# A decoder layer on one core: the weighting products as a stream of their own, a later read of x, an earlier mask load, and a changed account in the planner

## The chip, the core and the metric

The kernel runs on one core of one Trainium2 chip. The core has TensorE (matrix products, written into PSUM), VectorE, ScalarE and GpSimd (elementwise work and reductions), SyncE, which here only issues DMAs, and 16 DMA engines. The metric is the device time in microseconds, from one launch to its end. In the profile's rows PE is TensorE's products, PEld its weight loads, DVE is VectorE, ACT is ScalarE, POOL is GpSimd and SP is SyncE; a q behind a name (SPq) is that engine's sequencer.

## What is computed

A pre-norm decoder layer in float32 over x of shape (4, 1024, 256), with three residual parts. Cut to what matters:

```python
def attn(x):                     # 16 heads of 16, causal
    Q = (x @ Wq.T + bq).reshape(b, s, H, hd)
    K = (x @ Wk.T + bk).reshape(b, s, H, hd)
    V = (x @ Wv.T + bv).reshape(b, s, H, hd)
    Qt = einsum('bqhf,hfg->bqhg', Q, W_cross)
    K_mixed = einsum('hfg,bkhg->bkhf', M, K)     # M: shift_weights on diagonals
    scores = gt * (Qt . K) + (1 - gt) * (Q . K_mixed)
    attn = softmax(where(causal, scores * hd ** -0.5, -inf))
    return (attn @ V) @ Wo.T + bo

x = x + attn(layernorm(x))
x = x + cross_attention(layernorm(x), ctx, mask)   # 77 context rows, mask (4, 1024, 77)
x = x + w_down(silu(w_gate(n)) * w_up(n))          # n = layernorm(x), hidden 768, integer weights
```

## The kernel before

**Chunks.** The work goes in eight chunks, four batches b of two halves n, each of 512 rows (CH). Causality makes the second half of a batch cost twice the keys: n = 0 has 4 key blocks of 128, n = 1 has 8. Heads are taken in four groups of four (NG).

**Parts of a chunk.** `project` (L769) normalises the chunk's rows, transposes them and makes q, k and v. The rows of q and k are split into a rounded part and a remainder (hi, lo) and laid out by DMAs between parts of SBUF (`spread`, L713; eight DMAs at L727 for each half of q or of k, 128 KB each). `maxima` (L825) makes all scores once to find the row maxima: products at L853 and, on the diagonal, L861, reduced on VectorE at L866; `shift` (L732) turns the maxima. `attend` (L890) makes the scores again transposed, two pieces for each key block (L936, L942, diagonal L949), takes the exponential on ScalarE into an `es` buffer (L955), and weighs the values with it (L979, the inner function `weigh`). After the last key block of a group the sums are copied out (`normalise`, L659), transposed back and divided (`quotients`, L998; products at L668); after the last group the output projection follows (`out_proj`, L687; VectorE adds it to x at L711). `cross_attention` (L1043) and `ffn` (L1178) follow for the chunk; the FFN's products are at L1220 and L1254, and GpSimd makes the remainder of the hidden rows at L1231, into an `es` buffer too.

**Order of the weighing before.** `weigh` lags the scores by one key block, inside the attention stream: two score pieces, then the weighing of the block before them, and so on; quotients and output projection stand in the same stream, so that the scores of the next chunk come after the output projection of this one. x is read again (L906) for the residual sum when the chunk's attention begins; GpSimd adds the output bias to it (L909).

**Buffers.** PSUM has three `pair` buffers (scores, projections, FFN) and two `single` ones (sums). SBUF has six `es` buffers, two for each key block of a group, three `x` buffers, each held from the read of x to the end of the chunk's FFN, two `mk` buffers (masks) and the small ones.

**The order.** The prologue, up to L358, is in program order on every engine: weights come in on SP's and ScalarE's queues (L211 to L224), x01 (the second chunk's rows) last. Then a planner written into the kernel, `weave` (L458), orders TensorE's work while the program is built. Each part is a `Stream` of pieces; a piece states its TensorE time, the engines that it uses afterwards, the buffers that it takes and frees, a condition and an earliest time. `weave` always picks the piece that can start first in its account; streams that come first in the list win ties within 0.01 us, and a per-chunk list, LATES, shifts a stream's bids. A change of the array's shape (`mode`: rows of 64, columns of 32, whole) is charged 0.11 us. Once the maxima of the second group have begun ("begun"), only TensorE's order is written by the planner; before that VectorE's is too. The other engines' orders, SP's DMA issues among them, are the scheduler's own: it takes instructions in an order of its choice, ahead of their place in the program where nothing that they depend on holds them.

**Masks.** The mask of a batch is loaded by `load_mask` (L1013): the first in `late_weights` (L526, call at L532), the next ones in the cross attention. `load_cross` (L1017) reduces it (L1038) and scales it (L1040).

Of the kernel before, what the change touches and what calls it, by code (L numbers as in the profile page):

```python
# [8 lines left out]
F32 = mybir.dt.float32  # L9
# [3 lines left out]
U8 = mybir.dt.uint8  # L13
AF = mybir.ActivationFunctionType
ALU = mybir.AluOpType
# [4 lines left out]
P = 128  # L20
# [7 lines left out]
def tile_decoder_layer(  # L28
# [163 lines left out]


# [30 lines left out]
    x01 = x_rows(0, 1)  # L224

# [205 lines left out]
    tensor = {"end": 0.0, "mode": None}  # L431
# [26 lines left out]
    def weave(*streams, until=None):  # L458
        while True:
            live = [s for s in streams if s.next is not None]  # L460
            if not live or until in flags:
                return
            can = []
            for s in live:
                p = s.next
                if p["cond"] is not None and not p["cond"]():
                    continue
                t = max(
                    tensor["end"], p["at"], *(slots[k].when(c) for k, c in p["take"].items()), 0.0
                )  # L470
                if p["pe"] and p["mode"] != tensor["mode"]:
                    t += SWITCH
                if p["use"] and p["take"]:

                    eng, us = p["use"][0]
                    t = max(t, busy[eng].start(t + p["pe"], us) - p["pe"] - 1.0)
                if t < 1.0e8:
                    can.append((t + (s.lates[s.chunk] if s.lates else 0.0), t, s))
            assert can, [s.next for s in live]
            soon = min(c[0] for c in can) + WAIT  # L480
            _, t, s = next(c for c in can if c[0] <= soon)
            p = s.next
            s.got = {k: [slots[k].take() for _ in range(c)] for k, c in p["take"].items()}
            s.end = t + p["pe"]
            if p["pe"]:
                tensor.update(end=s.end, mode=p["mode"])
            for token in p["free"]:
                give(token, s.end)
            s.done = s.end
            for eng, us in p["use"]:  # L490
                s.done = busy[eng].run(s.done + LATE, us)
            s.next = next(s.pieces, None)
# [33 lines left out]
    def late_weights(st):  # L526
# [5 lines left out]
        load_mask(0)  # L532
# [236 lines left out]
    def project(st, b, n):  # L769
# [4 lines left out]
        else:  # L774
# [6 lines left out]
            normal_rows(xn, *row_scales(xn))  # L781
            yield piece(
# [6 lines left out]
        for c in range(NC):  # L789
# [8 lines left out]
            if c == 0:  # L798
                for i in range(QT):
                    if i % 2 == 0:  # L800
                        yield piece(
                            2.0, use=[("ACT", 1.8)] if i else [],
                            **({} if i else {"pair": 1, "v": 1}),
                        )
                        if i == 0:
                            t_pair, t_v = st.got["pair"], st.got["v"][0]
                            vs = qk.tile(
                                [P, QT, H * V1 + W - V1], F32, tag="v", name="vs", bufs=NQ
                            )
                            nc.gpsimd.memset(vs, 1.0)  # L810
                            t = pair().rearrange("p a (i d) -> p (a i) d", d=D)
# [77 lines left out]

    def attend(st, b, n):  # L890


        nat = t_nat = None
        nk = (n + 1) * QT
        lag = []
        tails = []
        for g in range(NG):
            c = g // 2
            if g % 2 == 0:
                yield piece(0.0, cond=lambda: (b, n, c) in shifts and (b, n) in vT and "selections" in flags)  # L900
                ms, at, t_ms = shifts.pop((b, n, c))
                if g == 0:
                    yield piece(0.0, x=1, use=[("DMA", 4.0)])
                    xt = xpool.tile([P, QT, D], F32, tag="x", name="x", bufs=3)
                    xs[b, n] = xt, st.got["x"][0]
                    nc.sync.dma_start(  # L906
                        xt, x[b, n * CH : (n + 1) * CH, :].rearrange("(t p) d -> p t d", p=P)
                    )
                    nc.gpsimd.tensor_tensor(  # L909
                        xt, xt, bo_b.unsqueeze(1).to_broadcast([P, QT, D]), ALU.add  # L910
                    )
# [4 lines left out]
            acc = []  # L916
            for kb in range(nk):
                kc, ki = divmod(kb, QT)
                k = kT[b, kc, c][0]
                vs, t_v, v_at = vT[b, kc]  # L920
# [4 lines left out]
                for p in range(2):  # L925
                    yield piece(
                        0.04 + w * 8.2e-4 + (0.11 if diag else 0.0), mode="rows", pair=1, es=1,
                        at=at,
                        use=[("ACT", 0.1 + w * 1.85e-3)],
# [29 lines left out]
                    ready = max(st.done + LATE, v_at)  # L959
                if g == 2 and n == NQ - 1 and kb == 0:  # L960
                    flags.add(("half", b))


                if g == NG - 1 and n == NQ - 1 and ki == QT - 1:
                    toks = toks + [t_v]

                def weigh(g=g, kb=kb, ki=ki, lo=lo, w=w, both=both, vs=vs, acc=acc, toks=toks,
                          ready=ready):
                    last = kb == nk - 1
                    yield piece(  # L970
                        0.03 + w * 1.77e-3, at=ready, free=toks, mode="cols",
                        use=[("ACT", 0.6)] if last else [],
                        **({"single": 1} if kb == 0 else {}), **({"f2": 1} if last else {}),
                    )
                    if kb == 0:
                        acc += [single(), st.got["single"][0]]
                    for jj in range(4):
                        h = 4 * g + jj
                        nc.tensor.matmul(  # L979
                            acc[0][W * jj : W * (jj + 1), lo:],  # L980
                            vs[:, ki, V1 * h : V1 * h + W], both[jj // 2][:, jj % 2, lo:],
                            start=(kb == 0), stop=last,
                        )
                    if last:
                        give(acc[1], st.done)
                        tails.append((normalise(acc[0]), st.got["f2"], st.done + LATE, g))

                lag.append(weigh)
                if len(lag) > 1:
                    yield from lag.pop(0)()  # L990
                if tails and kb == 1:
                    nat, t_nat = yield from quotients(st, tails.pop(), nat, t_nat)
        yield from lag.pop()()
        nat, t_nat = yield from quotients(st, tails.pop(), nat, t_nat)
# [16 lines left out]
    masks, mks = {}, {}  # L1011

    def load_mask(b):  # L1013
        mks[b] = xpool.tile([P, NT, S2], U8, tag="mk", name="mk", bufs=2)
        nc.sync.dma_start(mks[b], mask[b].rearrange("(t p) s -> p t s", p=P))
# [254 lines left out]
    def every(part, lates, chunks=range(NQ)):  # L1270
# [11 lines left out]
        [-0.05, 0.00, 0.00, 0.00, -0.09, 0.00, -0.11, 0.02],  # L1282
        [0.00, 0.00, -0.09, 0.00, 0.00, 0.00, 0.00, -0.48],
        [0.00, 0.00, 0.00, 0.00, 0.00, 0.00, 0.00, 0.00],
        [-3.63, 0.00, 0.00, 0.00],
        [0.74, 0.00, 0.00, 0.15],
        [0.00, -0.15, -0.34, 0.00, 0.00, 0.41, 0.00, 0.00],
    )
    streams = [
        every(maxima, LATES[0]), every(cross_attention, LATES[1]), every(attend, LATES[2]),  # L1290
        *(every(project, LATES[3 + n], [n]) for n in range(NQ)),
        Stream(late_weights), *(Stream(lambda st, m=m: load_ffn(st, m)) for m in range(3)),
        every(ffn, LATES[5]),
# [64 lines left out]
```

## Time and profile before

| what | us |
|---|---|
| median of 3 runs | 1239.33 (1238.6 to 1239.84) |
| profiled execution | 1236.36 |
| its span, first to last instruction | 1234.6 |
| TensorE busy | 1108.7 |
| VectorE busy | 729.8 |
| ScalarE busy | 561.2 |
| GpSimd busy | 130.5 |
| mean granted TensorE clock | 0.956 of full speed |
| 16 DMA engines, share of the span, SP's queue | 38.7% |

The costliest groups of instructions; the columns are line, engine, operation, output and inputs, shape, count, then busy time, mean ns of one, idle time of the engine just before them and what ended most of it:

```profile
L866 DVE TENSOR_REDUCE mt<-pair 128x2 f32<-128x1024 f32 (+3 forms) x384 | 352.6, 953 | 96.0 <-PE pair L861 60.8
L955 ACT ACTIVATE es<-pair 128x1024 f32<-128x1024 f32 (+3 forms) x384 | 300.2, 811 | 227.8 <-PE pair L949 158.1
L853 PE MATMUL pair<-k,q 64*128 64x512 f32 (+3 forms) x768 | 163.8, 432 | 39.9 <-DVE mt L866 15.1
L936 PE MATMUL pair<-q,k 64*128 64x512 f32 (+3 forms) x768 | 163.7, 423 | 18.5 <-DVE mt L866 9.7
L979 PE MATMUL single<-es,vs 128*32 128x512 f32 (+3 forms) x1536 | 163.3, 498 | 0.0
```

A busy time of TensorE is modelled at its end and is no proof of full speed; idle time of an engine that is not the bound costs nothing. The profile's slices and stretches give the granted clock beside the busy time, so that slow stretches can be told from empty ones.

### The profile page before, as it was taken

The numbers are of one execution on the slowest core, as the hardware profiler recorded it, in microseconds if no ns is written. First come the engines' busy times: TensorE is split into PE (matmuls) and PEld (weight loads), VectorE is DVE, ScalarE is ACT, GpSimd is POOL, SyncE is SP. The second block draws the span as 40 slices with busy tenths as digits, with TensorE's granted clock in tenths as the row PEclk, the third lists the DMA queues.
The fourth block names the chain that finished last, engine by engine and source line by source line (L and its number), as shares of the span: only waits on it lengthen the run. The fifth ranks groups of instructions, "written<-read, shape, count | busy, mean of one in ns | idle before, by whom it ended". The sixth has DMA issues, their size and how long they took to land. (4 is left out here: it accounts for less than half of the span.)

```text
span 1234.6 us, 22019 instructions
## 1 busy us (share of the span) xinstructions
PE 1108.7 (90%) x9059; PEld 683.7 (55%) x9059; DVE 729.8 (59%) x1247; ACT 561.2 (45%) x801; POOL 130.5 (11%) x138
## 2 busy tenths in 40 slices
PE   6489999999789999999899899899999899897975
PEld 4355545556556457557656456556656555456664
DVE  4577686254677867245777863652667746516443
ACT  3035455644343564653343555355344364572421
POOL 3230000001200003001200000201110000002112
PEclk9689999999999999999899899899899999998987
DMA  6973425457242014566533016363823314005000
GB/s 119 162 140 79 66 43 70 69 86 99 39 72 35 6 43 71 88 86 98 71 56 52 6 26 103 56 92 57 104 37 53 48 38 49 18 1 67 19 35 19
DMA packets 65437, 76.44 MB, mean 62 GB/s; under 512 B 22450, under 2 KB 39398, under 8 KB 65331
## 3 DMA queue, kind: packets, MB, share of 16 engines
q1 hardware_dynamic: 64227, 74.62, 38.7%
q8 instruction: 73, 1.20, 0.5%
q10 hardware_dynamic: 1104, 0.35, 0.1%
q14 instruction: 33, 0.27, 0.1%
HBM read 15.28 MB, written 9.33 MB: 20 GB/s over the span
## 5 line engine op out<-in xcount | busy, mean ns | idle before, releaser
L866 DVE TENSOR_REDUCE mt<-pair 128x2 f32<-128x1024 f32 (+3 forms) x384 | 352.6, 953 | 96.0 <-PE pair L861 60.8
L955 ACT ACTIVATE es<-pair 128x1024 f32<-128x1024 f32 (+3 forms) x384 | 300.2, 811 | 227.8 <-PE pair L949 158.1
L853 PE MATMUL pair<-k,q 64*128 64x512 f32 (+3 forms) x768 | 163.8, 432 | 39.9 <-DVE mt L866 15.1
L936 PE MATMUL pair<-q,k 64*128 64x512 f32 (+3 forms) x768 | 163.7, 423 | 18.5 <-DVE mt L866 9.7
L979 PE MATMUL single<-es,vs 128*32 128x512 f32 (+3 forms) x1536 | 163.3, 498 | 0.0
L853 PEld LDWEIGHTS pair<-k,q 64*128 64x128 f32 x768 | 76.8, 192 | 122.8 <-DVE mt L866 44.5
L942 PE MATMUL pair<-ms,sel 64*128 64x512 f32 (+3 forms) x768 | 135.8, 350 | 0.0
L936 PEld LDWEIGHTS pair<-q,k 64*128 64x128 f32 x768 | 73.5, 188 | 106.8 <-issue 38.4
L1231 POOL TENSOR_TENSOR hT<-h,hT 128x512 fp32r<-128x512 f32 x48 | 61.3, 1277 | 336.3 <-ACT hT L1230 310.4
L1153 ACT ACTIVATE es<-pair 77x1024 f32<-77x1024 f32 x64 | 63.1, 1018 | 35.6 <-PE pair L1151 35.1
L942 PEld LDWEIGHTS pair<-ms,sel 64*128 64x128 f32 x768 | 74.6, 191 | 2.8
L1254 PE MATMUL pair<-wdT,hT 128*128 128x256 f32 x384 | 61.9, 311 | 14.8 <-POOL hT L1231 4.1
L861 PE MATMUL pair<-cm_qk,id 64*128 64x64 bf16 (+1 forms) x1024 | 70.2, 214 | 0.0
L1226 ACT ACTIVATE h<-pair 128x512 f32<-128x512 f32 x48 | 28.6, 597 | 88.4 <-PE pair L1220 75.0
L949 PE MATMUL pair<-cm_kq,id 64*128 64x64 bf16 (+1 forms) x1024 | 67.0, 210 | 0.0
L1254 PEld LDWEIGHTS pair<-wdT,hT 128*128 128x128 f32 x384 | 53.8, 206 | 23.8 <-POOL hT L1231 5.2
L158 POOL TENSOR_TENSOR rs<-ve,mhalf 128x4 f32<-128x4 f32 x24 | 24.3, 1011 | 389.1 <-DVE ve L156 389.0
L1111 DVE TENSOR_REDUCE mx<-pair 128x8 f32<-128x616 f32 x64 | 48.4, 793 | 28.2 <-PE pair L1105 27.8
L1227 DVE SCALAR_TENSOR_TENSOR h<-h,pair 128x512 f32<-128x512 f32 x48 | 32.9, 684 | 54.0 <-ACT h L1226 50.0
L663 ACT COPY aS<-single 128x512 f32<-128x512 f32 x64 | 37.7, 588 | 45.5 <-PE single L1164 29.8
L190 ACT COPY xnT<-pair 128x1024 f32<-128x1024 f32 x32 | 32.5, 1014 | 48.8 <-PE pair L182 48.8
L979 PEld LDWEIGHTS single<-es,vs 128*32 128x32 f32 x1536 | 32.1, 108 | 39.7 <-issue 29.4
(180 smaller groups left out, 1589.9 us busy)
## 6 DMA issues: line engine op xcount, KB each, us to landing
q<-hi SPq DMA_DIRECT2D x128, 128.0 KB, 5.0
q<-lo SPq DMA_DIRECT2D x128, 128.0 KB, 6.0
k<-hi SPq DMA_DIRECT2D x64, 128.0 KB, 4.0
k<-lo SPq DMA_DIRECT2D x64, 128.0 KB, 6.3
xr<-in_x_dram SPq DMA_DIRECT2D x8, 512.0 KB
x<-in_x_dram SPq DMA_DIRECT2D x8, 512.0 KB, 7.1
x_dram<-x SPq DMA_DIRECT2D x8, 512.0 KB, 2.6
out_dram<-x SPq DMA_DIRECT2D x8, 512.0 KB, 3.9
```

Source lines behind the costliest of these rows:

```text
L853: nc.tensor.matmul(t[:, j, :w], q[r, a, i * P : (i + 1) * P], k[r, a, :w], start=True, stop=True,)
L861: nc.tensor.matmul(t[:, j, w - P + 64 * half : w], id2[r, half], cm_qk[r, half, 64 * half :], start=False, stop=True, skip_group_check=True,)
L866: nc.vector.tensor_reduce(mt[:, i, :, p, kc], t[:, :, :w], AX.X, ALU.max)
L936: nc.tensor.matmul(t[:, j, lo:], k[r, a, ki * P : (ki + 1) * P], q[r, a, lo:], start=True, stop=False,)
L942: nc.tensor.matmul(t[:, j, lo:], sel[r, hp, :], ms[r, lo:], start=False, stop=True)
L949: nc.tensor.matmul(t[:, j, lo : lo + 64 * (half + 1)], id2[r, half], cm_kq[r, half, : 64 * (half + 1)], start=False, stop=True, skip_group ...
L955: nc.scalar.activation(es[:, :, lo:], t[:, :, lo:], AF.Exp)
L979: nc.tensor.matmul(acc[0][W * jj : W * (jj + 1), lo:], vs[:, ki, V1 * h : V1 * h + W], both[jj // 2][:, jj % 2, lo:], start=(kb == 0), sto ...
L1111: nc.vector.tensor_reduce(mt[:, i, h4 : h4 + 4, :].rearrange("q (k p) j -> q k (p j)", k=2), tv[:, :, :, :S2], AX.X, ALU.max,)
L1153: nc.scalar.activation(es[:S2], t[:S2], AF.Exp)
L1231: nc.gpsimd.tensor_tensor(hs[:, 1, :], h, hs[:, 0, :].bitcast(F32), ALU.subtract)
L1254: nc.tensor.matmul(t[:, i, :], h[1][:, v, i * P : (i + 1) * P], w[:, h[0], :], start=(m == 0), stop=(m == len(terms) - 1),)
```

## The change

1. **Weighing as a stream.** The inner function `weigh` and its lag go. `attend` now only makes scores and exponentials and leaves each key block's `es` buffers, with the time at which they are ready, in a table `steps`. A new stream `weigh` takes them in order, makes the products, the quotients and the output projection, and sets the flag that lets the cross attention start. How far scores run ahead of the weighing is now bounded by the `es` buffers alone.
2. **x read late.** The read of x and GpSimd's addition move from the start of the chunk's attention to the first weighing of its last group. The piece also charges 1.5 us of POOL.
3. **First mask.** `load_mask` is defined before the prologue, and the first mask is loaded behind x01 on SP's queue; the call in `late_weights` goes.
4. **Values of the first chunk.** The value products of (0, 0) wait, in the planner's account, until the rows of (0, 1) are normalised.
5. **The account.** A piece that follows a pause of TensorE of more than 1.3 us is charged as if the clock were halved for the next 5 us.
6. **LATES.** New numbers, and one list more for the new stream.

No instruction of the computation is added, removed or resized.

```diff
+    mks = {}
+
+    def load_mask(b):
+        mks[b] = xpool.tile([P, NT, S2], U8, tag="mk", name="mk", bufs=2)
+        nc.sync.dma_start(mks[b], mask[b].rearrange("(t p) s -> p t s", p=P))
...
     x01 = x_rows(0, 1)
+    load_mask(0)
...
-    tensor = {"end": 0.0, "mode": None}
+    tensor = {"end": 0.0, "mode": None, "slow": 0.0}
+    REST, COLD = 1.3, 5.0
...
             if p["pe"]:
+                if t - tensor["end"] > REST:
+                    tensor["slow"] = t + COLD
+                s.end += min(max(tensor["slow"] - t, 0.0) / 2, p["pe"])
                 tensor.update(end=s.end, mode=p["mode"])
...
         flags.add("selections")
-        load_mask(0)
...
             normal_rows(xn, *row_scales(xn))
+            flags.add(("normal", b, n))
...
                             2.0, use=[("ACT", 1.8)] if i else [],
+                            cond=lambda: (b, n) != (0, 0) or ("normal", 0, 1) in flags,
...
     def attend(st, b, n):
...
-                if g == 0:
-                    yield piece(0.0, x=1, use=[("DMA", 4.0)])
-                    xt = xpool.tile([P, QT, D], F32, tag="x", name="x", bufs=3)
...
-                    ready = max(st.done + LATE, v_at)
+                    ready = max(ready, st.done + LATE)
+                steps[b, n, g, kb] = both, toks, ready
...
+    def weigh(st, b, n):
+
+        nat = t_nat = tail = None
+        nk = (n + 1) * QT
+        for g in range(NG):
+            for kb in range(nk):
+                yield piece(0.0, cond=lambda: (b, n, g, kb) in steps)
+                both, toks, ready = steps.pop((b, n, g, kb))
+                if kb == 0 and g == NG - 1:
+                    yield piece(0.0, x=1, use=[("DMA", 4.0), ("POOL", 1.5)])
+                    xt = xpool.tile([P, QT, D], F32, tag="x", name="x", bufs=3)
...
+                yield piece(
+                    0.03 + (CH - lo) * 1.77e-3, at=max(ready, v_at), free=toks, mode="cols",
+                    use=[("ACT", 0.6)] if last else [],
+                    **({"single": 1} if kb == 0 else {}), **({"f2": 1} if last else {}),
+                )
...
+                if kb == 1 and tail:
+                    nat, t_nat = yield from quotients(st, tail, nat, t_nat)
+                if last:
+                    give(t_acc, st.done)
+                    tail = normalise(acc), st.got["f2"], st.done + LATE, g
+        nat, t_nat = yield from quotients(st, tail, nat, t_nat)
         yield from out_proj(st, nat, t_nat, woT, xt)
         flags.add(("attended", b, n))
...
-        [-3.63, 0.00, 0.00, 0.00],
-        [0.74, 0.00, 0.00, 0.15],
-        [0.00, -0.15, -0.34, 0.00, 0.00, 0.41, 0.00, 0.00],
+        [0.00, 0.00, 0.00, 0.03, 0.00, 0.00, 0.00, 0.47],
+        [0.00, -0.71, -0.31, -0.43],
+        [0.00, 0.34, 0.14, 0.19],
+        [0.00, 0.00, 0.00, 0.00, 0.00, 0.73, 0.00, 8.32],
     )
     streams = [
-        every(maxima, LATES[0]), every(cross_attention, LATES[1]), every(attend, LATES[2]),
-        *(every(project, LATES[3 + n], [n]) for n in range(NQ)),
+        *(every(p, LATES[k]) for k, p in enumerate((maxima, cross_attention, attend, weigh))),
+        *(every(project, LATES[4 + n], [n]) for n in range(NQ)),
```

## The prediction

> **What bounds the kernel now.** The page first: the busy table, then the slices.
>
> ```profile
> span 1234.6 us, 22019 instructions
> ...
> PE 1108.7 (90%) x9059; PEld 683.7 (55%) x9059; DVE 729.8 (59%) x1247; ACT 561.2 (45%) x801; POOL 130.5 (11%) x138
> ...
> PE   6489999999789999999899899899999899897975
> ...
> PEclk9689999999999999999899899899899999998987
> DMA  6973425457242014566533016363823314005000
> ```
>
> TensorE bounds it: 8s and 9s nearly throughout. It is weak in the first two slices (0 to 62 us) and the last two (1173 to the end); single 8s with a lower clock between are stops, after which the clock is halved for a while. So a change can gain by filling stops or by taking TensorE work away. Second view, the waits of TensorE:
>
> ```profile
> PE pair L853 <- DVE mt L866: 15.1, 16, 8.6
> PE pair L853 <- DMA q<-lo: 12.2, 3, 11.0
> ```
>
> Columns: total us, times, longest. Two single waits, 11.0 and 8.6, make most of both rows. The timeline puts them at 27.4 to 38.3 and 50.7 to 59.4. What VectorE did in the second one:
>
> ```profile
> 47.39 0.69 DVE L517 COPY sel_f<-pm 128x1024 f32<-128x1024 f32 x1
> 56.58 0.80 DVE L1038 TENSOR_REDUCE keep<-mk 128x8 f32<-128x616 uint8 x1 [8.51 <-DMA mk<-in_mask_BxSxS_bk_dram]
> ...
> 58.88 0.42 DVE L866 TENSOR_REDUCE mt<-pair 128x2 f32<-128x256 f32 x1
> ```
>
> VectorE runs in order. The reduction of the first mask was put early in its queue, the mask was not there, and the maxima (L866) that free TensorE's pair buffers stood behind it. Why the mask was late: the DMA engines by stretch (PE, PEld, DVE, ACT, POOL busy, clock, DMA share, GB/s).
>
> ```profile
> 12.00:16.00 4.00, 4.00 (x19) 3.89 (x20) 1.64 (x6) 1.94 (x6) 2.19 (x6) 1.00 0.23 82
> 16.00:20.00 4.00, 4.00 (x12) 1.94 (x11) 0.84 (x2) 1.41 (x2) 3.35 (x9) 1.00 0.00 0
> 28.00:32.00 4.00, 0.00 (x0) 0.00 (x0) 2.74 (x9) 0.09 (x1) 2.43 (x4) 0.72 1.09 123
> 52.00:56.00 4.00, 0.00 (x0) 0.00 (x0) 0.00 (x0) 0.00 (x0) 0.00 (x0) 0.71 1.20 145
> ```
>
> From 20 us on, the q and k pieces fill the engines (over 1.0); from about 13.5 to 20 us they are empty. The issues on SP's queue:
>
> ```profile
> 49.50 0.37 SPq L1015 DMA_DIRECT2D mk<-in_mask_BxSxS_bk_dram  x1
> ...
> 51.42 0.37 SPq L906 DMA_DIRECT2D x<-in_x_dram  x1
> ...
> 76.38 0.37 SPq L906 DMA_DIRECT2D x<-in_x_dram  x1
> ```
>
> The mask was issued into the full stretch, 8 us behind its issue it was usable.
>
> **The change, part by part.**
>
> *First mask with the weights.* One DMA (77 KB) moves from 49.5 us to just behind x01, issued at 8.85; SP issues nothing from 9.2 to 19.57, so it delays no issue. It is 1024 packets of 77 bytes; in the trace these took 12 to 23 ns each, so 1024 x 15 ns / 16 engines = 1 us, into engines that are empty from 13.5 to 20. The Trainium skill (DMA: Bandwidth & Descriptors, Specifications) speaks against it: under 512 bytes a transfer is a read-modify-write. By the row it is 1 us; by the page's rule, taken as twice the time, an estimate, it is 2 us; the sum is the same by both. Gain: L1038 starts at 48.1 instead of 56.6, the first maxima behind it at 50.4 instead of 58.9: -8.5. What is late next: the maxima of chunk (0,1), begun at 88.3, which need q and k rows whose last DMA is issued at 70.5 to 73.0, with 6.0 to landing: 79.0. Moved 8.5 earlier they start at 79.8, a slack of 0.8. The full DMA engines could thus take back between 0 and 6.8 of it (6.8 if only the mask's own 1 us and the hole of 68 to 72, 4 us at 0.82, 0.7, are won); I take 1.5, near the end of none, to which the slack points. Sum: -7.0.
>
> *Clock of that stop.* The clock is halved from 53.7 to 67.3. The maxima there wait for VectorE, so only L755 (3.78 us for four matmuls at half, 1.88 at full at 25.48) is shortened: -1.9.
>
> *x01 normalised before the values of (0,0).* In the first weave VectorE's order is the program's: 7.6 us of L153 to L166 (27.07 to 34.67) move ahead of the second k remainder (26.40), which then ends near 30.4; its DMA is issued at 36.04, so 5.6 us of cover remain, without which it would cost 3.3. x01's transposes (1.97 at 44.78, with a wait of 1.10 behind) can go into the stop at 27.4 to 38.3. Between 0 and -3.1; I take -2.0, since the planner may still put them behind the maxima.
>
> *x read late.* The same eight loads and POOL adds. SP's order is the scheduler's: the x of the third chunk, whose scores start at 320.4, was issued at 76.4. Where a free buffer exists, the place in the program hardly sets the issue: between 0 and -3.5 (the megabyte of two x loads at the 298 GB/s of 56 to 60 us); I take 0. Late side: from the fourth group's first weighing to L711 there are at least 18.1 us (132.4 to 150.5), against 0.4 issue + 7.1 landing + 2.37 POOL = 9.9. If that cover went, L711 and the cross attention behind it would wait up to 9.9 us; behind the POOL add stand the hT differences (L1231, 1.28 each), and FFN products wait for those.
>
> *Weighing as a stream.* No instruction is added or removed: 192 steps of four products. In the trace 182 stand alone between other pieces and 5 times two follow each other: 187 runs.
>
> ```profile
> 1089.51 0.39 PE L942 MATMUL pair<-ms,sel 64*128 64x512 f32 x2
> 1089.74 0.40 PE L936 MATMUL pair<-q,k 64*128 64x512 f32 x2
> 1089.97 0.39 PE L942 MATMUL pair<-ms,sel 64*128 64x512 f32 x2
> 1090.29 1.07 PE L979 MATMUL single<-es,vs 128*32 128x512 f32 x8
> 1091.29 0.66 PE L668 MATMUL single<-ident,aS 128*128 128x128 f32 x4
> ```
>
> Score to score is 0.23 from start to start, score to weighing 0.32: +0.09. The two passes of one weighing step are 0.45 apart (median of single starts), the last one to the next shape 0.54: +0.09. A run costs 0.18 to 0.2. Six es buffers hold three steps, so runs could fall to 64: (187 - 64) x 0.2 = -24; none merged is 0, and a split pair or two more is +1. In the long stretch ACT's two exponentials (2 x 1.02) match TensorE's step (2 x 0.57 + 1.0), so scores rarely run ahead by themselves; nearest the end of none, about a ninth: 20 runs, -4.0.
>
> Second effect: quotients and output projection stood in the attention stream, so the next chunk's scores waited for them (138.5 to 150.5, 382.7 to 399.4, 663.4 to 682.4, 955.2 to 987.5). The stops over 0.6 us in these gaps add to 6.3, and 681.7 to 688.5 and 982.1 to 992.3 ran at half clock (17 us, 8.5 lost): 14.8 at most; a seventh, -2.0.
>
> *Stops in the account, new LATES.* These only reorder. From 84 to 1104 there are seven stops of 1.7 to 4.1 us (17.5) and 44 us at half clock (22): 39.5 at stake. Filled in part or added to: -10 to +10, I take 0, as neither sign shows. On the charge itself:
>
> ```profile
> 757.00:763.60 6.60, 4.89 (x26) 3.64 (x24) 3.40 (x6) 2.32 (x4) 2.02 (x2) 1.00 1.08 128
> 763.60:767.00 3.40, 3.40 (x23) 2.65 (x22) 1.88 (x3) 0.58 (x1) 0.52 (x1) 0.50 1.09 139
> ```
>
> A stop of 1.71 us at 761.19 was followed by 3.4 us at half clock, one of 2.01 at 1062.3 by none. The Trainium skill (TensorE: Matmul & The Clock Gate, What's actually happening) has the clock halved after an idle window of about 3.4 us; by it only the stops of 3.40 and 4.13 us would cost clock, the charge on the others would mislead the plan, and rival D would be worth a third of 17.5 and two such windows at half, (17.5 + 3.4) / 3 = 7 us, an estimate, in place of 13. The forecast's sum, with its 0 here, is the same by both.
>
> **Sum:** -7.0 - 1.9 - 2.0 + 0 - 4.0 - 2.0 + 0 = -16.9. The profiled execution took 1236.36 (span 1234.6), so 1219.5; the runs' median, 1239.33, lies 2.97 above it: 1222.4, said as 1222. The likeliest case's own range, with the bounds of its terms, is 1209 to 1230.
>
> **Rivals.**
> *A, the start alone:* runs are not merged, the gaps only move. For: es and ACT set the pace in both. -8.9 (mask and clock): 1230.
> *B, nothing:* DMA, at 1.05 and more until 84 us, takes the place of the mask wait, and only the 1.7 us named above leave the full stretch: 1238. Against: the first chunk's rows are all there by 52, and its scores are work enough.
> *C, slower:* scores run ahead and hold all six es buffers; the FFN, last in the list, needs one for each hT and falls behind, until one more of its chunks stands alone at the end. Now (3,1) does: 1187.7 to 1234.6 is 46.9 us with TensorE busy 26.0, 20.9 uncovered. A second one: -8.9 + 20.9 = +12.0: 1251. It decides once 8.9 of 20.9, some 43%, of the FFN of (3,0) falls behind the last L711 (1185.8). Against: three x buffers let no more than three FFN chunks be open, and three are at the end already.
> *D, the stops go too:* a third of 39.5 more: 1209 and below.
>
> **How the numbers follow.** The forecast 0.50, A 0.17, B 0.10, C 0.15, D 0.08. Range 1205 to 1241: it leaves out most of C and the far side of D. A measurement here tells no change within 0.2% (2.5 us: 1236.9 to 1241.8). Faster: forecast, D, A and a little of B: 0.76. Same: most of B: 0.08. Slower: C and a rest: 0.16.
>
> **What would show it.** Right: no wait of VectorE on mk before 60 us; longest wait of L853 on L866 under 2 us; the scores' first L936 before 70 (76.6 now); fewer runs of L979 than 160; x01's transposes before 38. Wrong: rows of q or k awaited by TensorE between 60 and 90; waits for es at L1231 or L1254 and an FFN of (3,0) behind 1186; more stops over 1.7 us than seven between 84 and the last attention.

## The result, and the profile after

The changed kernel took 1255.09 us, the median of four runs (1252.12 to 1255.21); the kernel before, in the same batch of runs, 1238.96. The ratio is 1.0126, interval 1.0109 to 1.0142: 16 us slower. The profiled execution took 1255.04 us, its span 1253.3. The page of the kernel after, busy table and slices:

```profile
span 1253.3 us, 22044 instructions
...
PE 1119.9 (89%) x9059; PEld 692.9 (55%) x9059; DVE 727.4 (58%) x1247; ACT 561.0 (45%) x801; POOL 131.0 (10%) x138
...
PE   6597889998899799899989899999999999997875
...
PEclk9699899999899899899989799989999989998888
DMA  6956205337470350065562301911475314005000
```

TensorE is still the bound and issues the same 9059 products. PE has an 8 or a 7 in 12 slices (11 before), and PEclk in 12 (8 before). The costliest groups, by their new line numbers (maxima 866, their reduction 879, scores 937, exponential 956, weighing 999):

```profile
L956 ACT ACTIVATE es<-pair 128x1024 f32<-128x1024 f32 (+3 forms) x384 | 298.8, 812 | 240.5 <-PE pair L950 155.0
L879 DVE TENSOR_REDUCE mt<-pair 128x2 f32<-128x1024 f32 (+3 forms) x384 | 351.8, 953 | 87.5 <-PE pair L874 59.9
L866 PE MATMUL pair<-k,q 64*128 64x512 f32 (+3 forms) x768 | 167.0, 438 | 37.0 <-DVE mt L879 11.9
L937 PE MATMUL pair<-q,k 64*128 64x512 f32 (+3 forms) x768 | 160.8, 415 | 26.9 <-DVE mt L879 17.9
L999 PE MATMUL single<-es,vs 128*32 128x512 f32 (+3 forms) x1536 | 164.7, 515 | 0.0
```

Work on VectorE and ScalarE is unchanged; what grew is the scores' idle time, 18.5 to 26.9, put down to the reductions. TensorE's waits (us in total, times, longest):

```profile
PE pair L937 <- DVE mt L879: 17.9, 19, 8.0
PE pair L866 <- DVE mt L879: 11.9, 23, 2.2
PE pair L866 <- DMA q<-lo: 10.8, 5, 8.1
...
PE pair L655 <- POOL wi L641: 7.3, 1, 7.3
```

The 8.6 us behind the mask are gone (the longest of L866 is now 2.2), but two stops of 8.0 and 7.3 us have come.

**Where the 18.7 us of span went.** Three sums split a span. Idle is span less TensorE's busy time. The clock is granted at 1.00 or 0.50, so the time at half clock can be had from the mean (before: 2 x (1 - 0.956) x 1234.6 = 109). Half of what TensorE was busy in that time is lost. The rest is work at full clock.

| us | span | idle | at half clock | busy time lost to it | work at full clock |
|---|---|---|---|---|---|
| before | 1234.6 | 125.9 | 109.1 | 38.8 | 1069.9 |
| after | 1253.3 | 133.3 | 144.7 | 56.1 | 1063.8 |
| change | +18.7 | +7.4 | +35.6 | +17.3 | -6.1 |

The work did fall, by 6.1. Stops and the clock behind them took four times that back. By stretch, before and after: up to 70 us idle 30.1 and 26.2, half clock 30.7 and 27.3; from there to the end of the last attention's scores (1103.0 and 1115.1) idle 66.1 and 72.9, half clock 47.8 and 81.9; behind it idle 29.7 and 34.2, half clock 30.6 and 35.5. The start is better, the long middle worse, above all in clock. The first score starts at 68.2 instead of 76.6, but the last scores of the first chunk end at 142.4, not 138.5: the gain of the start was spent by then.

**The two long stops.** First, TensorE's timeline (start, length, engine, line, operation; idle before it and its releaser in brackets), then SP's and GpSimd's:

```profile
118.78 0.61 PE L655 MATMUL pair<-ident,wi 128*128 128x128 f32 x4
126.70 1.12 PE L655 MATMUL pair<-ident,wi 128*128 128x128 f32 x4 [7.30 <-POOL wi L641]
```

```profile
107.34 2.86 SPq L1034 DMA_DIRECT2D k2s<-k_dram  x4
...
112.06 7.54 SPq L1034 DMA_DIRECT2D k2s<-k_dram  x12
...
120.28 0.54 SPq L639 DMA_DIRECT2D wi<-in_L_ffn_w_up_dram  x1
```

```profile
125.60 3.10 POOL L641 CAST wi<-wi 128x1024 f32<-128x1024 int32 x4 [15.40 <-DMA wi<-in_L_ffn_w_up_dram]
```

TensorE's order, fixed by the planner, has transposes of FFN weights here. Their load stands in SP's queue behind sixteen loads for the cross attention, is issued at 120.28, and GpSimd's cast (the conversion of the integer weights) starts only at 125.60, when it has come. VectorE before the second stop:

```profile
422.21 1.23 DVE L722 TENSOR_TENSOR x<-pair,x 128x1024 f32<-128x1024 f32 x1 [6.67 <-PE pair L717]
423.93 1.22 DVE L722 TENSOR_TENSOR x<-pair,x 128x1024 f32<-128x1024 f32 x1 [0.50 <-PE pair L717]
...
428.99 1.38 DVE L166 TENSOR_SCALAR xn<-x,mv,rs 128x256 f32<-128x256 f32 x4 [0.95 <-POOL rs L160]
...
432.31 1.38 DVE L166 TENSOR_SCALAR xn<-x,mv,rs 128x256 f32<-128x256 f32 x4 [1.12 <-POOL rs L158]
433.61 1.22 DVE L879 TENSOR_REDUCE mt<-pair 128x2 f32<-128x1024 f32 x1
```

Two residual sums end close together, and two normalisations, each with a wait on GpSimd, stand in VectorE's queue ahead of one maximum, whose buffer the next scores need. What each stop leaves behind it, by stretch (PE, PEld, DVE, ACT, POOL busy, clock, DMA share, GB/s):

```profile
122.10:132.40 10.30, 5.70 (x40) 2.98 (x40) 3.68 (x6) 1.17 (x2) 5.87 (x6) 0.50 0.75 244
...
429.30:439.60 10.30, 4.72 (x20) 2.11 (x22) 5.20 (x14) 1.02 (x1) 1.01 (x1) 0.50 0.01 2
```

The clock falls some 2.5 us into the stop and stays halved for 10.3: 5.70 and 4.72 us of products ran at half speed, which is 2.9 and 2.4 us more for each stop.

### The profile page after: what moved, and what is told of

Read it like the earlier page. It is cut to its first block, busy times and chain, and to the rows that moved or that the text cites. A ratio compares the mean times of both kernels' runs of the same rounds, so it can differ in the third digit from the quotient of the medians.

```text
span 1253.3 us, 22044 instructions
## 1 busy us (share of the span) xinstructions
PE 1119.9 (89%) x9059; PEld 692.9 (55%) x9059; DVE 727.4 (58%) x1247; ACT 561.0 (45%) x801; POOL 131.0 (10%) x138
## 5 line engine op out<-in xcount | busy, mean ns | idle before, releaser
L879 DVE TENSOR_REDUCE mt<-pair 128x2 f32<-128x1024 f32 (+3 forms) x384 | 351.8, 953 | 87.5 <-PE pair L874 59.9
L866 PE MATMUL pair<-k,q 64*128 64x512 f32 (+3 forms) x768 | 167.0, 438 | 37.0 <-DVE mt L879 11.9
L937 PE MATMUL pair<-q,k 64*128 64x512 f32 (+3 forms) x768 | 160.8, 415 | 26.9 <-DVE mt L879 17.9
L866 PEld LDWEIGHTS pair<-k,q 64*128 64x128 f32 x768 | 78.2, 195 | 132.8 <-DVE mt L879 48.8
L937 PEld LDWEIGHTS pair<-q,k 64*128 64x128 f32 x768 | 73.7, 189 | 99.8 <-issue 27.1
L1241 POOL TENSOR_TENSOR hT<-h,hT 128x512 fp32r<-128x512 f32 x48 | 61.3, 1278 | 359.1 <-ACT hT L1240 323.8
L1264 PE MATMUL pair<-wdT,hT 128*128 128x256 f32 x384 | 58.9, 305 | 7.9 <-ACT hT L1240 3.6
L684 DVE RECIPROCAL rd<-single 128x16 f32<-128x16 f32 x64 | 16.2, 253 | 76.1 <-PE single L679 76.0
L1264 PEld LDWEIGHTS pair<-wdT,hT 128*128 128x128 f32 x384 | 52.2, 203 | 13.5 <-ACT hT L1240 4.3
L999 PEld LDWEIGHTS single<-es,vs 128*32 128x32 f32 x1536 | 35.3, 111 | 43.8 <-issue 33.1
```

The costliest lines, as they stand in the source:

```text
L866: nc.tensor.matmul(t[:, j, :w], q[r, a, i * P : (i + 1) * P], k[r, a, :w], start=True, stop=True,)
L879: nc.vector.tensor_reduce(mt[:, i, :, p, kc], t[:, :, :w], AX.X, ALU.max)
L937: nc.tensor.matmul(t[:, j, lo:], k[r, a, ki * P : (ki + 1) * P], q[r, a, lo:], start=True, stop=False,)
L999: nc.tensor.matmul(acc[W * jj : W * (jj + 1), lo:], vs[:, ki, V1 * h : V1 * h + W], both[jj // 2][:, jj % 2, lo:], start=(kb == 0), stop=last,
L1241: nc.gpsimd.tensor_tensor(hs[:, 1, :], h, hs[:, 0, :].bitcast(F32), ALU.subtract)
L1264: nc.tensor.matmul(t[:, i, :], h[1][:, v, i * P : (i + 1) * P], w[:, h[0], :], start=(m == 0), stop=(m == len(terms) - 1),)
```

## The experiments

All comparisons are with the kernel before, in the same batch of runs. "Account" is the program's own sum over its plan, not a time of the chip.

**The mask alone (e1), and with the late read of x (e5)**, in the old order of TensorE. e1:

```diff
     x01 = x_rows(0, 1)
+    load_mask(0)
...
         flags.add("selections")
-        load_mask(0)
```

> The kernel before with one edit: the first mask is loaded behind x01 and not in late_weights; TensorE's order stays that of before. Theory (the mask pays, the new order loses it and more): VectorE no longer waits 8.5 us on mk, the longest wait of the maxima's products on their reductions falls from 8.6 to under 2 us, and nearly all stays: 1231, between 1229 and 1234. Rival (the start is given back whatever the order, because DMA engines are full until 84 us): 1237 to 1239, with a new wait on q or k rows or on weight loads between 60 and 130 us.

e5 moves the read and GpSimd's sum of x besides:

```diff
-                    xt = xpool.tile([P, QT, D], F32, tag="x", name="x", bufs=3)
...
+                    if kb == 0 and g == NG - 1:
+                        xt = xpool.tile([P, QT, D], F32, tag="x", name="x", bufs=3)
```

> The run with the early mask, and besides x is read at the first weighing of the last group instead of at the start of the attention; TensorE's order is again that of before. Theory (the place of the read hardly matters while a buffer is free): within 2 us of the run with the early mask alone. Rival (the late read is what costs, through the output projection's sum waiting for x and GpSimd's queue): 5 us or more above it, with waits of the sum (DVE x) on GpSimd. Second rival (1 MB less in the full stretch helps): 3 us below it.

e1 took 1231.11 us, ratio 0.9936 (0.9907 to 0.9966); e5 1230.74, 0.9937 (0.9918 to 0.9956). The mask's reduction in e1, on VectorE:

```profile
47.21 0.79 DVE L1040 TENSOR_REDUCE keep<-mk 128x8 f32<-128x616 uint8 x1
```

No wait before it, where there were 8.51 us. In the old order the mask is worth some 8 us (by the ratio, 4 to 12), in line with the forecast of 7.0 and 1.9 for the clock. The late place in the program changed nothing that could be seen: SP issued the first three reads of x at 50.34, 54.15 and 74.29 us in e5, and at 50.34, 54.16 and 74.34 in e1. So e5 shows that the place hardly sets the issue, as forecast; what a truly late read costs it doesn't test.

**The same two parts taken out of the change: the mask (e2) and the late read (e6).** In e2 `load_mask(0)` returns to `late_weights`; in e6:

```diff
+                if g == 0:
+                    xt = xpool.tile([P, QT, D], F32, tag="x", name="x", bufs=3)
+                    early[b, n] = xt
...
-                    xt = xpool.tile([P, QT, D], F32, tag="x", name="x", bufs=3)
+                    xt = early.pop((b, n))
```

> The changed kernel with the first mask loaded in late_weights again; TensorE's order stays that of the changed kernel. Theory (the mask pays 8 us in both orders, and the rest of the change costs 24): 1263, between 1260 and 1266, with the 8 us wait of VectorE on mk back. Rival (in the changed order the early mask is worth nothing, the next stop takes its place): 1255 to 1257.

> The changed kernel with x read at the start of the chunk's attention again (the planner takes the buffer at the same place as in the changed kernel, so TensorE's order stays). Theory (the order alone loses): 1253 to 1257. Rival (the late read costs): 1250 or less, and the stop of 7.3 us at 119 us, where TensorE waits for an FFN weight that GpSimd converts, gone or below 3 us.

e2: 1255.08, ratio 1.012 (1.0086 to 1.0154), the time of the change. SP's queue and VectorE in e2:

```profile
40.17 0.37 SPq L197 DMA_DIRECT2D mk<-in_mask_BxSxS_bk_dram  x1
```

```profile
49.09 0.80 DVE L1048 TENSOR_REDUCE keep<-mk 128x8 f32<-128x616 uint8 x1 [0.46 <-DMA mk<-in_mask_BxSxS_bk_dram]
```

In the changed order SP issues the mask at 40.17 even from its old place (49.50 before), and the reduction waits 0.46 for it. So the early mask, worth some 8 us in one order, is worth little or nothing in the other: the medians are equal, within an interval of some 4 us, and in the profiles e2 runs 2 to 3 us behind the change from 98 to 1000 us. e6: 1250.6, 1.011 (1.0053 to 1.0166), 4.5 less than the change, but the intervals overlap and its stop at 121.5 is still 6.7 long: not told apart.

**One long stop removed (e7): the FFN weights on ScalarE's queue.**

```diff
-            nc.sync.dma_start(wi, rows)
+            nc.scalar.dma_start(wi, rows)
```

> The changed kernel with the FFN's weight loads (L639) issued on ScalarE's queue instead of SP's; TensorE's order stays that of the changed kernel. Theory (the loads stand on SP behind the 16 loads of the cross keys, and TensorE's transposes of them, which the planner put early, wait): the wait of TensorE on GpSimd's conversion at 119 us falls from 7.3 to under 2 us, the 10 us at half clock behind it go, and the time falls by 7 to 12: 1243 to 1248. Rival (the start is full anyway and the stop moves): the stop goes and another of the same size comes before 160 us; 1252 to 1256.

1255.79 (1251.55 to 1259.54), ratio 1.0158 (1.0115 to 1.0201). TensorE's waits:

```profile
PE pair L937 <- DVE mt L879: 19.7, 19, 8.0
...
PE pair L937 <- ACT es L956: 4.4, 11, 0.6
```

The row of L655 is no longer among the long ones, as both theories had it, and the time is the same. Stops of 2.78 (at 116.8), 1.84 (147.0) and 1.52 us (222.9) came instead. TensorE issues its products in the same order in both kernels, so they can be compared one by one: the 801st starts at 136.8 here and at 136.9 in the change, and the 1001st at 167.9 instead of 165.0. The time of the long stop was lost again within 20 us: other waits took its place.

**The other long stop (e8): VectorE's order from the planner too**, in the change, and, as a control, in e1 (e9).

```diff
-    with tc.manual_schedule(engines={ENG.PE}):
+    with tc.manual_schedule(engines={ENG.PE, ENG.DVE}):
```

> The changed kernel with VectorE's order, too, taken from the planner for the whole of the work (before, only until the second group's maxima); TensorE's order stays. Theory (the plan is sound and loses because VectorE's queue, which the scheduler orders, holds two normalisations ahead of a reduction that TensorE needs): the stop of 8.0 us at 427 us goes and the time falls by 8 or more, to 1247 or less. Rival (VectorE in the plan's order waits in line for GpSimd and ScalarE in each normalisation and each hidden row, and more is lost): 1265 or more.

> The kernel before with the early mask, and VectorE's order taken from the planner throughout. Theory (the older plan has few places where VectorE's order hurts): within 5 us of 1231. Rival (an order of VectorE that follows the plan is good or bad in itself, whatever the plan): the same sign and size of difference as in the changed kernel.

e8: 1257.48, 1.0164 (1.0133 to 1.0196). Its wait of L937 on L879:

```profile
PE pair L937 <- DVE mt L879: 16.8, 19, 6.0
```

The 8.0 is gone, but one of 6.0 at 124.9 stands there, and others of 5.2 (532.0) and 4.4 (1162.2) are new. By its interval e8 is not told apart from the change; it lies between the two forecasts. e9: 1246.21, 1.008 (1.005 to 1.0111), 1.4% over e1, more than either theory had. In these two orders the planner's order is no better for VectorE than the scheduler's.

**Is it the stream, the charge, or the new list? (d1 to d4.)** d1 and d2 have e1's structure (no stream, no charge) and other numbers in LATES, as good in the account. d3 and d4 have the stream without the charge, and other numbers, equal in the account and 5 us better.

```diff
-        [-3.63, 0.00, 0.00, 0.00],
+        [0.08, 0.00, 0.00, -0.24],
...
-    REST, COLD = 1.3, 5.0
+    REST, COLD = 1.0e9, 5.0
```

> The weighing inside the attention stream as before, the early mask, no charge on stops; LATES replaced by another list, found by a random search until the planner's own account was as good as with the list of before. All of TensorE's order is new. Theory P (what a plan is worth on the chip depends on where its stops fall, not on its kind: lists that the account holds equal scatter over 20 us): somewhere between 1228 and 1252, and not near its twin. Theory W (the weighing as a stream costs some 20 us by itself, whatever the list): 1228 to 1236, like the early mask alone.

> As the run before, with a second list found from another start, as good in the account. Theory P: between 1228 and 1252, apart from its twin by 5 or more. Theory W: 1228 to 1236.

> The changed kernel without the charge on stops (the weighing as a stream, x late, mask early, values behind x01's normalisation all kept); LATES another list, as good in the account as that of before. Theory P: between 1228 and 1255, like the lists with the weighing in the attention stream. Theory W: 1248 to 1260. Theory C (the charge on stops is what spoils the plan): 1228 to 1238.

> As the run before with a second list, better in the account than any of the others by 5 us or more. Theory P: between 1225 and 1250, not ahead of the others by its account. Theory W: 1243 to 1256. Theory C: 1222 to 1232.

| | median us | ratio | interval |
|---|---|---|---|
| d1 | 1261.53 | 1.0196 | 1.0156 to 1.0237 |
| d2 | 1251.48 | 1.0119 | 1.0078 to 1.0161 |
| d3 | 1262.01 | 1.0206 | 1.0158 to 1.0253 |
| d4 | 1263.16 | 1.0197 | 1.0145 to 1.0249 |

Three of the four (d1, d3, d4) came out above every range that was named for them. A new list alone, with neither stream nor charge, costs as much as the whole change: by the ratios d1 and d2 stand 2.6% and 1.8% over e1 (32 and 23 us), the change 1.9%. Without the charge the stream is no better. In the old structure, what sets before apart is its list: of the three lists there that the account rates alike, it runs best on the chip. Whether the stream costs something of its own can't be read from this: the two new lists of the old structure alone stand 10 us apart, and 23 and 32 us from e1.

**The clock of the early stop (e10).** To e1 it adds 22 products of 128x512 whose result nothing reads, in the wait of 11 us for q and k.

```diff
+            for _ in range(22):
+                nc.tensor.matmul(t, ident, wqT.rearrange("p a b -> p (a b)"), start=True, stop=True)
```

> The kernel before with the early mask, and 22 products of 128x512 without use, written to a buffer that nobody reads, between the last projection of the first chunk and the first maxima, where TensorE waits 11.0 us for q rows; the rest of TensorE's order stays. In the run with the early mask the clock was halved from 32.2 to 45.8 and from 52.7 to 59.5, and 6.8 us of busy time were lost to it in the first 62 us. Theory (halved clock costs time of its own, apart from the stop): the first of the two windows goes, the products fill some 9.5 of the 11 us, and the time falls by 2 to 6: 1225 to 1229. Rival (the maxima there wait for VectorE and the DMA engines, so the clock is free): 1230 to 1233, or a little more if the products delay the first maxima.

1231.38, ratio 0.9932 (0.9898 to 0.9966): e1's time. But the edit did more than fill the wait. The stretch's start in e10, then in e1:

```profile
26.62 19.15 PE L833 MATMUL single<-wqT,ident 128*128 128x512 f32 x44
45.71 0.33 PE L863 MATMUL pair<-k,q 64*128 64x128 f32 x2
```

```profile
38.20 0.44 PE L859 MATMUL pair<-k,q 64*128 64x128 f32 x1 [11.04 <-DMA q<-lo]
```

The 22 products stand in the trace as 44 records, 0.43 us apart, and took 19.15 us, not the 9.5 that were planned. The first maxima came 7.5 us later than in e1, behind the useless products and no longer behind q. The same stretch of time in e10, then in e1:

```profile
32.20:45.80 13.60, 13.60 (x34) 5.80 (x32) 2.63 (x4) 0.00 (x0) 1.50 (x3) 1.00 1.08 133
```

```profile
32.20:45.80 13.60, 6.65 (x54) 6.05 (x55) 8.39 (x12) 0.00 (x0) 1.89 (x3) 0.50 1.08 125
```

The clock was full, as meant. From there, mostly at full clock and with the rows already there, the maxima made up some 4 of the 7.5 us by 61 us. The rest went later: the same stops, of 1.82 us (at 190.4 in e1) and 1.89 us (589.0), halved the clock in e1 and not in e10, where they came 4.0 and 2.0 us later. So the equal times don't show that the full clock was worth nothing in this stretch; its price there stays open.

**Does the account say anything? (e11, e12, e13, e14, e15.)** e11 is the change with one number of LATES moved, 26 us worse in the account; e12 the stream alone, with before's list, 70 us worse.

```diff
-        [0.00, 0.34, 0.14, 0.19],
+        [0.00, 0.34, 0.14, 0.24],
```

> The changed kernel with one number of LATES altered by 0.05 (the last one of the second half's projections, 0.19 to 0.24), which makes the planner's own account worse by 26 us. Theory P (the account's differences of this size are mostly not the chip's): within 12 us of 1255. Rival (the account is sound apart from an offset, which was larger for the changed kernel): 1275 to 1287.

> The weighing as a stream, alone: the list of before with zeros for the new stream, no charge on stops, mask and x where they were before, values of the first chunk unbound. The planner's own account is worse by 70 us than that of before, as this list was found for the other kind of stream. Theory P (the account's differences shrink on the chip, and no list that was not chosen on the chip does as well as that of before): 1260 to 1290. Rival (the account is right): 1304 or more. Second rival (the stream is a gain that the new list spoils): 1239 or less.

e11: 1270.26, 1.0248 (1.0219 to 1.0277), 15 over the change, between the two forecasts. e12: 1325.82, 1.0686 (1.0656 to 1.0717), 85 over before, with 181 us of idle and 192 at half clock; here the account was right, and theory P wrong. Large differences in the account are real. For small ones, near lists, in which some numbers differ slightly: e13 and e14 from e1 (11 and 8 us better in the account), e15 from the change (7 better). e13:

```diff
-        [-0.05, 0.00, 0.00, 0.00, -0.09, 0.00, -0.11, 0.02],
-        [0.00, 0.00, -0.09, 0.00, 0.00, 0.00, 0.00, -0.48],
-        [0.00, 0.00, 0.00, 0.00, 0.00, 0.00, 0.00, 0.00],
-        [-3.63, 0.00, 0.00, 0.00],
-        [0.74, 0.00, 0.00, 0.15],
-        [0.00, -0.15, -0.34, 0.00, 0.00, 0.41, 0.00, 0.00],
+        [-0.05, 0.00, -0.02, -0.04, -0.12, 0.00, -0.16, 0.02],
+        [0.00, 0.00, -0.09, 0.00, -0.22, 0.01, 0.01, -0.48],
+        [0.00, 0.00, 0.00, 0.00, 0.00, 0.00, 0.00, 0.11],
+        [-3.63, 0.00, 0.01, 0.09],
+        [0.74, 0.14, 0.00, 0.15],
+        [-0.12, -0.12, -0.06, 0.09, 0.07, 0.41, 0.00, 0.00],
```

> The early mask with the weighing in the attention stream, and LATES moved in 16 places, by less than 0.25 nearly everywhere, so that the planner's own account ends 11 us earlier than with the list of before. Theory P (differences of this size in the account are not the chip's, and the list of before is one that does well on the chip): slower than the early mask alone, 1233 to 1255. Rival (near one good list the account's gain is real): 1218 to 1226, and then a version better than both kernels by far.

> As the run before with a second list near that of before, 8 us better in the account. Theory P: 1233 to 1255. Rival: 1220 to 1228.

> The changed kernel with a list near its own, 7 us better in the account, which charges the stops. Theory P (the changed kernel's list is an ordinary one, so that its neighbours are no worse than it): 1245 to 1262. Rival (the account's gain is real): 1246 to 1250. If the stream with the charge can do as well as the early mask in the older order, 1235 or less would be seen here.

e13: **1216.91**, ratio 0.9824 (0.9793 to 0.9855), the best of all kernels here, 20 us under before and, by the ratios, 14 under e1, against theory P. e14: 1233.72, 0.9966 (0.9949 to 0.9984), no gain over e1. e15: 1247.21, 1.0076 (1.0055 to 1.0098), 0.5% under the change. Two of three small gains held, one did not. The page of e13:

```profile
span 1215.5 us, 22024 instructions
...
PE 1100.2 (91%) x9059; PEld 678.6 (56%) x9059; DVE 728.3 (60%) x1247; ACT 561.7 (46%) x801; POOL 130.4 (11%) x138
...
PE   6689999999989899999897998899999899997975
...
PEclk9699999999999999999899999899999999998986
```

Its waits on the maxima's reduction have no single long one, and neither have those of e1 (1.8 and 1.2 the longest):

```profile
PE pair L942 <- DVE mt L872: 13.3, 22, 1.8
PE pair L859 <- DVE mt L872: 12.8, 29, 1.2
```

By the three sums e13 has idle 115.4, busy time lost 30.8 and work 1069.3. Against the change that is -17.9, -25.3 and +5.5, against e1 -6.5, -6.2 and -1.1: the order decides by stops and clock, not by work.

## Why the prediction was wrong

**The step that failed** is "Stops in the account, new LATES. These only reorder ... -10 to +10, I take 0, as neither sign shows." With the order went more than its own stops. In the stretch from 70 us to the last scores idle time rose by 6.8 us and the busy time lost to half clock from 21.7 to 34.3. Forecast and profiled change (-16.9 and +18.7) differ by 35.6. The mask and its clock account for 8.9 (forecast -8.9, taken as worth 0 in this order by e2). The work at full clock fell by 2.1 more than the 4.0 forecast for shape changes. What is left, some 29 (35.6 - 8.9 + 2.1), belongs by subtraction to the order and to the small terms that hang on it, three times the bound. I took the old order as one among equals; d1 and d2 show that another list costs 23 to 32 us in the old structure. The planner fixes TensorE's order alone; the orders of SP, VectorE and GpSimd are the scheduler's, and both long stops came from what stood in those queues.

**First mask: right in its mechanism, wrong in its use.** e1 measured some -8 (by the ratio, -4 to -12) against -8.9 for the mask and its clock. But the sum added it to a new order, in which SP issued the mask 9 us earlier anyway. Rival B's thought, that something hides the gain, held, by another cause than the one named.

**x01 earlier: seen, gain not measured.** Its transposes run at 26 to 30 us, as said. But the first maxima start at 38.2 as before, since they wait for q rows; what the transposes left free later was not measured by itself.

**x late: as forecast where the issue didn't move.** Nothing in e5, where SP issued the reads when it did before. In the change the second and third reads were issued at 122.5, where before they were issued at 55.5 and 76.4; e6 leaves open whether that costs anything.

**Fewer runs of weighing: right in number, price open.** 161 runs instead of 187, where 167 were forecast (and under 160 as a sign). Work fell by 6.1; 26 fewer runs would be 0.23 each, if all of it were theirs. But other lists don't bear the price out: e12 has 150 runs and 1071.1 us of work at full clock, d3 174 and 1076.4, d4 172 and 1079.0, all more than before's 1069.9 with 187.

**Scores of the next chunk no longer behind quotients: the mechanism is there, the gain is not.** The gaps between the last score of a chunk and the first of the next add to 82.7 us instead of 173.5, and TensorE's idle time in them to 5.5 instead of 16.9. Yet idle time from 70 us to the last scores rose by 6.8: the stops came elsewhere.

**The rivals.** C had the side but not the cause. GpSimd waited once at L1241 for a weighing to end, 12.6 us at 777 to 790 (before, two such waits on TensorE, of 8.8 and 7.4), but no product of L1264 waited for GpSimd more than 1.0, and the FFN of (3,0) is over at 1203.1, before the last L722 at 1206.6. D, that stops go, is the opposite of what happened: the stops over 1.7 us from 84 to the last attention add to 26.2 us instead of 19.3, with 7.97 and 7.30 as the longest instead of 4.13, and the time at half clock is up by 34 from 70 us on. Their number did not rise. The prediction counted seven before and left out one of 1.85 at 679.5; there were eight before and there are eight after. So its sign of "wrong", more than seven, told nothing: the kernel before met it too. What grew was the size of two.

**Not settled.** Which part of the 29 is the stream's and which the list's. e13 and e15, the better near lists of both structures, stand 30 us apart, and all ten kernels here with the stream are slower than before, which speaks for a price of the stream. But the lists of the old structure scatter as far (1217 to 1262), so the rival that the stream itself costs 10 us or more is neither shown nor ruled out.

## What to carry to other kernels

A change that makes a planner order an engine anew is not neutral: first measure two or three other orders that the plan rates alike in the old kernel; their scatter (here 23 to 32 us above the kept list) belongs into the range of the prediction. Price a removed wait in the order that the change will have, not in the one where it was seen, and expect a mended stop to be lost again elsewhere while the other engines' queues stay in an order that the plan doesn't know. When the plan's rating is trusted only for large differences, run several near orders and keep the best: here the best of three near orders gained 14 us over the early mask alone, where the change lost 16 against the kernel before.

## What the runs showed of the hardware

**The clock goes by a grid.** In every profile taken here the stretches of granted clock 0.50 begin and end on one grid of 3.41 us, so they last 3.4, 6.8, 10.2 or more (only the last one of a profile is cut short, by its end). Stops of TensorE between 70 us and 150 us before the end, over the 19 profiles, that did not begin at half clock: of those of 3.4 us or more all 34 were followed by a halved stretch (beginning no later than 4 us after them), of those from 1.7 to 3.4 us 81 of 101, of those from 1.0 to 1.5 us 36 of 87.

What tells better than one stop is TensorE's idle time, long and short stops added, within one step of the grid. Of the steps at full clock in the same part of the 19 profiles, many of which share an order, none of 4642 with under 0.6 us of idle was followed by a halved step; of those with 0.6 to 1.7 us, 68 of 594; with 1.7 to 1.9, 42 of 46; with 1.9 or more, all 87. So several short stops in one step halve the clock too, which the change's charge on single stops over 1.3 us doesn't see, and what one stop costs hangs on where in the grid it falls. The stop of 1.71 us in the prediction lay within one step, the one of 2.01 left 1.68 in its step; and the stops of 1.82 and 1.89 named at e10 halved the clock in one run and not in the other.

The Trainium skill (TensorE: Matmul & The Clock Gate, What's actually happening) tells of a free-running window of about 3.4 us and an idle one that halves the clock; the step agrees, but here most stops of half a window to a whole one (the 81 of 101) were followed by half clock as well.

**A full stretch of DMA.** Spreading rows between parts of SBUF held the DMA engines at 1.08 with 125 to 133 GB/s (the two rows of e10 and e1), while the loads of weights and of x at 122 to 132 us moved 244 GB/s at 0.75. A packet of 2 KB of the first kind took 275 ns (median, e1), one of 1 KB of the second 47: busy engines are no measure of bytes moved.
